# Two graph attentions on one core: the end of the first one, with norm weights folded into matrices and evictions moved between engines

## The chip, the cores and the metric

The kernel runs on one core of one Trainium2 chip. A core has four compute engines with an instruction queue each, worked off in order: TensorE (PE in the profile; its weight loads are PEld), VectorE (DVE), ScalarE (ACT) and GpSimd (POOL). SyncE (SP) only issues DMAs here. Engines wait for each other through semaphores. The metric is the device time of one execution in microseconds, and the median of several.

## The reference

A graph of N = 1250 nodes and E = 20000 edges, with 768 features a node, goes through two graph layers, each behind a layer norm and a residual. The first layer holds two attentions (GATv2), and the change touches the passage from one to the other:

```python
def gatv2(x, src, dst, Ws, bs, Wd, bd, attn):        # attn: H heads x D
    fs = (x @ Ws + bs).reshape(-1, H, D)
    fd = (x @ Wd + bd).reshape(-1, H, D)
    e = leaky_relu(fs[src] + fd[dst], 0.2)
    logits = einsum('ehd,hd->eh', e, attn)
    ex = exp(logits - segment_max(logits, dst)[dst])
    alpha = ex / segment_sum(ex, dst)[dst]
    return elu(segment_sum(alpha[:, :, None] * fs[src], dst))

h   = gatv2(x, src, dst, W1s, b1s, W1d, b1d, attn1)   # 8 heads of 96
h   = layer_norm(h + x, ln1_w, ln1_b)                 # (v - mean) * rsqrt(var + eps) * w + b
out = gatv2(h, src, dst, Wos, bos, Wod, bod, attno)   # 1 head of 768
x   = layer_norm(out, lno_w, lno_b)
```

Here `x` is max(norm(input), 0), and the result is added to the input. The second layer is a relational graph convolution (34 relations, each with a 768 x 768 matrix) followed by a graph convolution; the change does not touch it.

## The kernel before

**Stages.** By the profile's times: edge lists and the two products of the first attention up to about 260 us, the first attention to about 905, the second to 1370, the relations to 2567, the graph convolution to the end at 2808.5. The stages follow each other, since each reads tables that the last tile of the stage ahead has written.

**Tiles and slots.** Nodes are sorted by their number of incoming edges and cut into ten tiles of 128 (`k` = 0 to 9). Tile k has as many slots as its busiest node has edges: 33, 22, 20, 18, 17, 16, 15, 14, 13 and 11, 179 in all. A slot is one incoming edge of each of the 128 nodes. Tiles of over 20 slots are worked in two chunks.

**A slot** has a front and a back. The front (`front`): POOL gathers the 128 source rows by an indirect DMA into one of a ring of 24 buffers (L1145, `fs<-f_fs_d` in the first attention, `fs<-r_fs_d` in the second). VectorE takes `z = max(fs, nfd)` (L1205), multiplies by the attention vector (L1210) and sums by head (L1211). Leaky relu is split there: 0.2 (fs + fd) is linear, so its sum with the attention vector comes with the source row, in extra columns ("quarter sums", because SLOPE / (1 - SLOPE) is 0.25), and the rest is 0.8 max(fs + fd, 0), which is 0.8 (max(fs, -fd) + fd). `nfd` is the tile's -fd; its own sums are the same for all edges of a node, and the softmax takes them out. The back (`back`): ScalarE scales the gathered row by the softmax weight, one instruction for each of eight heads (L1263), and TensorE adds it to the tile's PSUM sum by two matmuls with the identity (L1265, `ag`). A buffer of the ring is free again when the ag matmuls of its slot are done. The loop at the foot of `attention` works the back of one chunk and the front of the next side by side; `softmax` stands between them (exponential L1229).

**POOL's second work.** With each gather of the first attention, 0.9 scatters of list records are issued (L1149, `r_pair_d<-rec,place`); what is left over of the 179, up to 60, follows the last gather. The relations read these lists.

**A tile's beginning.** `negated1`, called one chunk or two ahead, gathers the nodes' own rows h0, transposes them, multiplies by W1d (L1114, PSUM tag mm2) and evicts `nfd = -(product + b1d)` on VectorE (L1409).

**A tile's end.** `end` multiplies the sum by 1/denominator (`share`) and takes elu (L1288 to L1290). Then `finish1`, as long as the change finds it:

```python
            nc.vector.tensor_add(o, o, h0s.pop(k))
            sc, sh = norm_scale(nc, small, f, o, P)
            nc.scalar.activation(o, o, AF.Identity, bias=sh, scale=sc)        # L1418
            nc.vector.tensor_mul(o, o, lnw)                                   # L1419
            nc.vector.tensor_add(o, o, lnb)                                   # L1420
            ...
            nc.vector.tensor_add(halves(fs, P, f), ps[:, :, :HW], halves(bias_s, P, f))    # L1426
            ...
            nc.vector.scalar_tensor_tensor(wt, fs[:, :D], SLOPE / (1.0 - SLOPE), attn_o, op0=ALU.mult, op1=ALU.mult,
                                           accum_out=fs[:, D:])               # L1428
```

The normed rows are transposed on TensorE (`to_columns`), multiplied by Wos, evicted with the bias into `fs2` (one buffer) with the quarter sum as a 769th column, and scattered by POOL into the table `r_fs_d` of the second attention (L1149, `r_fs_d<-fs,f_perm`). Then the product with Wod is evicted as `-(product + bod)` on VectorE (L1433) and stored by SyncE. All products of `negated1` and `finish1` use one PSUM buffer, mm2.

**The weights.** `loads1` is called at the front of the fourth slot: Wos and Wod come by SyncE's queue (issued at 239.0 and 239.5 us), the rows lnw, lnb, bias_s, bias_d and attn_o, each spread over 128 partitions, by ScalarE's.

**Order.** The order in each engine's queue is not written out by hand: a scheduler merges the instruction streams, so instructions of `finish1`, of slots and of `negated1` interleave on each engine.

Of the kernel before, what the change touches and what calls it, by code (L numbers as in the profile page):

```python
# [10 lines left out]
F32 = mybir.dt.float32  # L11
# [3 lines left out]
AF = mybir.ActivationFunctionType  # L15
ALU = mybir.AluOpType
AX = mybir.AxisListType

P = 128
# [606 lines left out]
def fast_front(ctx, tc, f, x, src, dst, edge_type, W1s, b1s, W1d, b1d, attn1, attno, W_rel):  # L626
# [51 lines left out]
    with ExitStack() as front:  # L678
# [33 lines left out]
        ones_row = early.tile([1, P], F32, name="ones_row")  # L712
# [10 lines left out]
        f.bias_1 = const.tile([P, D], F32, name="bias_1")  # L723
        nc.scalar.dma_start(f.bias_1, bass.AP(tensor=b1d.tensor, offset=b1d.offset, ap=[[0, P], [1, D]]))
# [352 lines left out]
def halves(t, n, f):  # L1077
    return t[:n, :f.D].rearrange("p (a b) -> p a b", a=2)
# [45 lines left out]
def fast_rest(ctx, tc, f, x, src, dst, edge_type, W1s, b1s, W1d, b1d, attn1, ln1_w, ln1_b,  # L1124
# [44 lines left out]
    def attention(H, table, negated, attn_e, first, loads, finish, rate, rest):  # L1169
# [98 lines left out]
        def share(o, ps, by):  # L1268

            if H == 1:  # L1270
                nc.vector.tensor_scalar(halves(o, P, f), ps[:, :, :HW], by, None, op0=ALU.mult)
            else:
                nc.vector.tensor_tensor(
                    o.rearrange("p (a h d) -> p a h d", a=2, d=HD),
                    ps[:, :, :HW].rearrange("p a (h d) -> p a h d", d=HD),
                    by.rearrange("p (a h) -> p a h", a=2)[:, :, :, None].to_broadcast([P, 2, H // 2, HD]),
                    op=ALU.mult)

        def end(t):
# [4 lines left out]
            share(o, c.ps, c.den)  # L1284
# [3 lines left out]
            nc.vector.tensor_scalar(e, o, 0.0, None, op0=ALU.min)  # L1288
# [31 lines left out]
        for j, now in enumerate(chunks):  # L1320
# [13 lines left out]
            if now.first + now.n == now.t.S:  # L1334
# [7 lines left out]
                            f.degf[:, :, None].to_broadcast([P, NT, S0]), op=ALU.is_ge)  # L1342

# [46 lines left out]
    with ExitStack() as one:  # L1390
        bias_1 = f.bias_1
# [10 lines left out]
        def negated1(k, nfd):  # L1402

            h0s[k] = pool.tile([P, D], F32, name="h0", tag="h0r", bufs=3)
            gather(h0s[k], f.h0_d[:, :], f.permg[:, k:k + 1])
            hT = pool.tile([P, KC, P], F32, name="hT0", tag="hT1", bufs=1)
            to_columns(nc, ps_t, f, hT, 0, h0s[k], P, both=True)
            ps = dense(nc, ps_t, f, hT, f.w1d, 0, P, tag="mm2")
            nc.vector.scalar_tensor_tensor(  # L1409
                nfd.rearrange("p (a h) d -> p a h d", a=2), ps[:, :, :HW].rearrange("p a (h d) -> p a h d", d=D // H),  # L1410
                -1.0, bias_1.rearrange("p (a h d) -> p a h d", a=2, d=D // H), op0=ALU.mult, op1=ALU.subtract)

        def finish1(k, o):
            lnw, lnb, wos, wod = late["lnw"], late["lnb"], late["wos"], late["wod"]
            bias_s, bias_d, attn_o = late["bias_s"], late["bias_d"], late["attn_o"]
# [3 lines left out]
            nc.vector.tensor_mul(o, o, lnw)  # L1419
            nc.vector.tensor_add(o, o, lnb)  # L1420
            hT = pool.tile([P, KC, P], F32, name="hT1", tag="hT1", bufs=1)
            to_columns(nc, ps_t, f, hT, 0, o, P)
            ps = dense(nc, ps_t, f, hT, wos, 0, P, tag="mm2")
            ap1 = late["pool"]
            fs = ap1.tile([P, W2], F32, name="fs2", tag="fs2", bufs=1)
            nc.vector.tensor_add(halves(fs, P, f), ps[:, :, :HW], halves(bias_s, P, f))  # L1426
            wt = work.tile([P, D], F32, name="wt2", tag="att_e")
            nc.vector.scalar_tensor_tensor(wt, fs[:, :D], SLOPE / (1.0 - SLOPE), attn_o, op0=ALU.mult, op1=ALU.mult,  # L1428
                                           accum_out=fs[:, D:])
# [3 lines left out]
            nc.vector.scalar_tensor_tensor(halves(fd, P, f), ps[:, :, :HW], -1.0, halves(bias_d, P, f),  # L1433
                                           op0=ALU.mult, op1=ALU.subtract)
# [5 lines left out]
    with ExitStack() as two:  # L1440
# [34 lines left out]
        attention(1, fs2_d, negated2, f.attn_o, lambda: None, loads2, finish2, 0, 0)  # L1475
# [239 lines left out]
```

## Time and profile before

| what | us |
|---|---|
| median of three runs | 2816.5 (2815.39 to 2821.32) |
| the profiled execution | 2810.31 |
| its span | 2808.5 |
| granted TensorE clock, mean | 0.932 of full speed |
| first attention, tiles running | 263 to 873 |
| of its 610 us busy: PE, DVE, ACT, POOL | 488.3, 538.6, 418.4, 477.0 |
| last list scatter of the first attention to the first gather of the second | 872.7 to 905.9 |

The slices of the page cut the span into 40 equal parts of 70 us; a digit is the busy share in tenths, 9 for 90% and more:

```profile
PE   6942684789898386889599999999999999997998
DVE  5579979898994999999463433343333333310000
ACT  3003774776762122333212122212212212221000
POOL 1332877787884776776374555455455544421000
```

The first attention is the stretch of the fourth to the thirteenth digit, in which all four engines are in use; the second attention follows with a busy DVE; in the relations PE is the one at 9. A group line has the line of the code, engine, operation, output and inputs with their shapes, and a count; then the sum and the mean in us and ns; then the idle time just ahead of the group's instructions and what ended it. A timeline line begins with its start and its length in us. Register, semaphore and DMA-issuing instructions do not count as busy. All times that follow are of this profiled execution, which lies 6.2 us below the median.

### The profile page before, as it was taken

To read this page: it belongs to the slowest core of one execution; us is meant where nothing else is said; L and a number is where in the kernel's file an instruction comes from. 1 tells how busy PE (TensorE), PEld (TensorE's weight loads), DVE (VectorE), ACT (ScalarE), POOL (GpSimd) and SP (SyncE) were. 2 spreads that over 40 slices of the span, in tenths; PEclk is the share of its full clock that TensorE was granted. 3 is DMA by queue.
4 is the path that set the end of the run, shared out by engine and by line. 5 is a ranking of instruction groups with operands and counts; after the bars stand their busy time and mean duration, and the time that the engine had idled before them with its cause. 6 is when DMAs were issued, how large, how long until landed. Compare 5 with 4: busy or idle time off the path is not lost. (4 is left out here: it accounts for less than half of the span.)

```text
span 2808.5 us, 24226 instructions
## 1 busy us (share of the span) xinstructions
PE 2396.5 (85%) x7859; PEld 1395.3 (50%) x7859; DVE 1615.1 (58%) x2382; ACT 852.6 (30%) x2340; POOL 1471.1 (52%) x1039
## 2 busy tenths in 40 slices
PE   6942684789898386889599999999999999997998
PEld 3521252445454243545366666666666666664455
DVE  5579979898994999999463433343333333310000
ACT  3003774776762122333212122212212212221000
POOL 1332877787884776776374555455455544421000
PEclk9976997999999698999799999999999999999999
DMA  6144443444431766675477777777677777665211
GB/s 213 46 157 156 134 132 91 125 145 134 133 97 53 277 206 189 212 220 169 169 196 214 191 185 197 184 187 186 181 201 186 184 201 198 174 147 136 75 45 51
DMA packets 130769, 447.82 MB, mean 159 GB/s; under 512 B 25016, under 2 KB 27601, under 8 KB 130634
## 3 DMA queue, kind: packets, MB, share of 16 engines
q0 software_dynamic: 77792, 305.26, 41.7%
q1 hardware_dynamic: 48041, 133.96, 13.4%
q10 hardware_dynamic: 4800, 6.96, 0.7%
q8 instruction: 65, 1.06, 0.2%
q14 instruction: 71, 0.57, 0.1%
HBM read 357.08 MB, written 89.11 MB: 159 GB/s over the span
## 5 line engine op out<-in xcount | busy, mean ns | idle before, releaser
L1114 PE MATMUL ps<-wrel,mT 128*128 128x384 f32 x3336 | 1099.4, 486 | 1.2 <-DMA wrel<-in_L_gnn_W_rel_dram 1.2
L1114 PEld LDWEIGHTS ps<-wrel,mT 128*128 128x128 f32 x3336 | 623.2, 190 | 407.4 <-issue 1.5
L1145 POOL DMA_INDIRECT g<-r_h_d,lists x241 | 365.9, 1518 | 474.1 <-DVE g L1566 302.3
L1265 PE MATMUL ag<-fs,identf 128*128 128x384 f32 x716 | 290.2, 539 | 173.2 <-ACT fs L1263 163.4
L1263 ACT ACTIVATE fs<-fs,lg 128x96 f32<-128x96 f32 x1376 | 370.6, 362 | 2.4 <-issue 1.9
L1566 DVE TENSOR_TENSOR g<-g,g 128x768 f32<-128x768 f32 x68 | 64.6, 949 | 526.4 <-DMA g<-r_h_d,lists 464.7
L1205 DVE TENSOR_TENSOR z<-fs,nfd 128x776 f32<-128x776 f32 (+1 forms) x358 | 344.0, 976 | 39.6 <-DMA fs<-f_fs_d,srci 22.6
L1255 PE MATMUL ag<-fs,dg 128*128 128x384 f32 x716 | 252.3, 514 | 86.2 <-ACT dg L1253 45.9
L1145 POOL DMA_INDIRECT fs<-f_fs_d,srci x179 | 245.9, 1374 | 103.1 <-issue 47.2
L1592 POOL DMA_INDIRECT r_h_d<-y,lists x139 | 227.3, 1635 | 133.1 <-ACT y L1591 65.8
L1149 POOL DMA_INDIRECT r_pair_d<-rec,place x179 | 240.9, 1346 | 101.3 <-DVE lg L1211 48.6
L1265 PEld LDWEIGHTS ag<-fs,identf 128*128 128x128 f32 x716 | 135.2, 204 | 315.7 <-ACT fs L1263 247.5
L1145 POOL DMA_INDIRECT fs<-r_fs_d,srci x179 | 242.5, 1355 | 82.6 <-PE ag L1255 35.5
L1506 DVE SCALAR_TENSOR_TENSOR arow<-node,from_f,arow 128x1250 f16<-128x1250 f16 x179 | 270.7, 1514 | 3.7
L1255 PEld LDWEIGHTS ag<-fs,dg 128*128 128x128 f32 x716 | 142.9, 202 | 190.8 <-ACT dg L1253 91.1
L1591 ACT COPY y<-ps 128x768 f32<-128x768 f32 x71 | 56.8, 799 | 482.0 <-PE ps L1114 482.0
L1589 ACT ACTIVATE y<-ps,rcnt 128x768 f32<-128x768 f32 x68 | 61.3, 902 | 444.4 <-PE ps L1114 444.4
L1207 DVE SCALAR_TENSOR_TENSOR z<-z,attn_o 128x769 f32<-128x769 f32 x179 | 180.2, 1027 | 0.0
L1210 DVE TENSOR_TENSOR z<-z,attn 128x776 f32<-128x776 f32 x179 | 168.3, 954 | 0.1
L1211 DVE TENSOR_REDUCE lg<-z 128x8 f32<-128x776 f32 x179 | 167.9, 950 | 0.1
L1647 DVE COPY gT<-hb 128x512 f32<-128x512 f32 (+1 forms) x9 | 5.4, 603 | 250.0 <-ACT gT L1646 250.0
L1643 PE MATMUL hb<-adj,h 125*128 125x512 f32 (+1 forms) x360 | 130.9, 526 | 14.6 <-DMA h<-r_h_d 14.6
(274 smaller groups left out, 2269.7 us busy)
## 6 DMA issues: line engine op xcount, KB each, us to landing
wrel<-in_L_gnn_W_rel_dram SPq DMA_DIRECT2D x37, 2304.0 KB
g<-r_h_d,lists POOLq DMA_INDIRECT x241
r_nfd_d<-fd SPq DMA_DIRECT2D x10, 384.0 KB
nfd<-r_nfd_d SPq DMA_DIRECT2D x10, 384.0 KB
r_x_d<-xb SPq DMA_DIRECT2D x10, 384.0 KB
x1r<-r_x_d SPq DMA_DIRECT2D x10, 384.0 KB
f_fs_d<-o_s SPq DMA_DIRECT2D x9, 388.0 KB
x<-in_x_dram SPq DMA_DIRECT2D x9, 384.0 KB
```

Source lines behind the costliest of these rows:

```text
L1114: last = nc.tensor.matmul(ps[:n, half, :f.HW], hT[:, k, j * P:j * P + n], w[:, k, cols], start=(k == 0), stop=(k == f.KC - 1 and not bias))
L1145: return nc.gpsimd.indirect_dma_start(out=to, out_offset=None, in_=table, in_offset=bass.IndirectOffsetOnAxis(ap=idx, axis=0))
L1149: s = nc.gpsimd.indirect_dma_start(out=table, out_offset=bass.IndirectOffsetOnAxis(ap=idx, axis=0), in_=rows, in_offset=None, **kw)
L1205: nc.vector.tensor_tensor(z, fs, t.nfd, op=ALU.max)
L1207: nc.vector.scalar_tensor_tensor(z[:, 0, :], z[:, 0, :], 1.0, attn_e[:, 0, :], op0=ALU.mult, op1=ALU.mult, accum_out=t.lg[:, s, :])
L1210: nc.vector.tensor_mul(z, z, attn_e)
L1211: nc.vector.tensor_reduce(t.lg[:, s, :], z, axis=AX.X, op=ALU.add)
L1255: nc.tensor.matmul(c.ps[:, half, :HW], dg, fs[:, 0, half * HW:(half + 1) * HW], start=begin, stop=end)
L1263: nc.scalar.activation(fs[:, h, :HD], fs[:, h, :HD], AF.Copy, scale=t.lg[:, s, h:h + 1])
L1265: nc.tensor.matmul(c.ps[:, half, :HW].rearrange("p (h d) -> p h d", d=HD), f.identf, fs[:, half * H // 2:(half + 1) * H // 2, :HD], start= ...
L1506: nc.vector.scalar_tensor_tensor(a, node16, from_f[:, k, s:s + 1], a, op0=ALU.is_equal, op1=ALU.add)
L1592: s = nc.gpsimd.indirect_dma_start(out=h1_d[:, :], out_offset=bass.IndirectOffsetOnAxis(ap=j.node, axis=0), in_=y, in_offset=None, compute ...
```

## The change

The norm of the first attention, `w * n + b` with n the plain normed row, is followed only by the products with Wos and Wod. So w can be multiplied into the rows of the two matrices once, and b becomes a row, `b @ W`, that joins the layer's own bias. The change does this in `loads1`, on the loaded matrices: ScalarE scales their blocks, TensorE computes the bias rows. The bias of the source product (`bos + b @ Wos`) is not added to the rows of the table any more; since the softmax weights of a node sum to one, it is added after the weighted sum, in the second attention's `share`, and it cancels from the logits but for the maximum: as it stands within max(fs, -fd), it goes into the destination's bias, by the third product below (`sums[:, 0]`). The quarter sums become a 769th column of Wos (six sums on VectorE, once). A node without edges would have the bare bias now, so the second attention's norm is multiplied by a 0/1 column (`f.has`). The evictions of nfd, fs (in halves) and fd go from VectorE to ScalarE, and the biases of nfd and fd come as one more matmul of a ones row for each half.

```diff
-        f.bias_1 = const.tile([P, D], F32, name="bias_1")
+        f.bias_1 = const.tile([1, D], F32, name="bias_1")
...
-        def share(o, ps, by):
+        def share(o, ps, by, bias=None):
-            if H == 1:
+            if bias is not None:
+                nc.vector.scalar_tensor_tensor(halves(o, P, f), ps[:, :, :HW], by, halves(bias, P, f),
+                                               op0=ALU.mult, op1=ALU.add)
+            elif H == 1:
...
+    f.has = rp.tile([P, NT], F32, name="has")
+    nc.vector.tensor_scalar(f.has, f.degf, 0.5, None, op0=ALU.is_gt)
...
         def loads1():
-            late["wos"], late["wod"] = load_w(ap1, Wos, "wos", "wos"), load_w(ap1, Wod, "wod", "wod")
-            for name, a in (("lnw", ln1_w), ("lnb", ln1_b), ("bias_s", bos), ("bias_d", bod), ("attn_o", attno)):
-                late[name] = load_row(ap1, a, name)
+            wos = late["wos"] = ap1.tile([P, KC, W2], F32, name="wos")
+            nc.sync.dma_start(wos[:, :, :D], Wos.rearrange("(k p) n -> p k n", p=P))
+            wod = late["wod"] = load_w(ap1, Wod, "wod", "wod")
...
+            for i, a in enumerate((ln1_w, ln1_b)):
+                nc.scalar.dma_start(cols[:, i, :], bass.AP(tensor=a.tensor, offset=a.offset, ap=[[1, P], [P, KC]]))
+            for i, a in enumerate((bos, bod)):
+                nc.scalar.dma_start(rows[:, i, :], bass.AP(tensor=a.tensor, offset=a.offset, ap=[[0, 1], [1, D]]))
+            late["bias_d"] = sums[:, 1, :]
+            for i, w in enumerate((wos, wod)):
+                ps = ps_t.tile([P, 2, 512], F32, name="b_ps", tag="mm2")
+                for half in range(2):
+                    at = slice(half * HW, (half + 1) * HW)
+                    for k in range(KC):
+                        nc.tensor.matmul(ps[:1, half, :HW], cols[:, 1, k:k + 1], w[:, k, at], start=(k == 0), stop=False)
+                    if i:
+                        nc.tensor.matmul(ps[:1, half, :HW], f.ones_row[:, :1], sums[:, 0, at], start=False, stop=False)
+                    nc.tensor.matmul(ps[:1, half, :HW], f.ones_row[:, :1], rows[:, i, at], start=False, stop=True)
+                nc.scalar.copy(sums[:, i, :].rearrange("p (a b) -> p a b", a=2), ps[:1, :, :HW])
+                for k in range(KC):
+                    nc.scalar.activation(w[:, k, :D], w[:, k, :D], AF.Copy, scale=cols[:, 0, k:k + 1])
+            ps = ps_t.tile([P, 2, 512], F32, name="b_ps", tag="mm2")
+            for half in range(2):
+                nc.tensor.matmul(ps[:, half, :HW], f.ones_row, sums[:, 0, half * HW:(half + 1) * HW], start=True, stop=True)
+            nc.scalar.copy(halves(f.bias_s, P, f), ps[:, :, :HW])
+            for k in range(KC):
+                wt = work.tile([P, D], F32, name="wt2", tag="att_e")
+                nc.vector.scalar_tensor_tensor(wt, wos[:, k, :D], SLOPE / (1.0 - SLOPE), f.attn_o[:, 0, :D],
+                                               op0=ALU.mult, op1=ALU.mult, accum_out=wos[:, k, D:])
...
-            ps = dense(nc, ps_t, f, hT, f.w1d, 0, P, tag="mm2")
-            nc.vector.scalar_tensor_tensor(
+            ps, _ = dense(nc, ps_t, f, hT, f.w1d, 0, P, tag="mm2", bias=(f.ones_row, f.bias_1))
+            nc.scalar.activation(
                 nfd.rearrange("p (a h) d -> p a h d", a=2), ps[:, :, :HW].rearrange("p a (h d) -> p a h d", d=D // H),
-                -1.0, bias_1.rearrange("p (a h d) -> p a h d", a=2, d=D // H), op0=ALU.mult, op1=ALU.subtract)
+                AF.Copy, scale=-1.0)
...
-            nc.vector.tensor_mul(o, o, lnw)
-            nc.vector.tensor_add(o, o, lnb)
...
-            nc.vector.tensor_add(halves(fs, P, f), ps[:, :, :HW], halves(bias_s, P, f))
-            wt = work.tile([P, D], F32, name="wt2", tag="att_e")
-            nc.vector.scalar_tensor_tensor(wt, fs[:, :D], SLOPE / (1.0 - SLOPE), attn_o, op0=ALU.mult, op1=ALU.mult,
-                                           accum_out=fs[:, D:])
+            for half in range(2):
+                at = slice(half * HW, HW if half == 0 else W2)
+                for c in range(KC):
+                    nc.tensor.matmul(ps[:, half, :at.stop - at.start], hT[:, c], wos[:, c, at], start=(c == 0), stop=(c == KC - 1))
+                nc.scalar.copy(fs[:, at], ps[:, half, :at.stop - at.start])
...
-            ps = dense(nc, ps_t, f, hT, wod, 0, P, tag="mm2")
+            ps, _ = dense(nc, ps_t, f, hT, wod, 0, P, tag="mm2", bias=(f.ones_row, late["bias_d"]))
...
-            nc.vector.scalar_tensor_tensor(halves(fd, P, f), ps[:, :, :HW], -1.0, halves(bias_d, P, f),
-                                           op0=ALU.mult, op1=ALU.subtract)
+            nc.scalar.activation(halves(fd, P, f), ps[:, :, :HW], AF.Copy, scale=-1.0)
...
+            for a in (sc, sh):
+                nc.vector.tensor_mul(a, a, f.has[:, k:k + 1])
```

More of the change, by code (lines that the diff above doesn't have):

```diff
@@ L711, in fast_front @@
         nc.scalar.dma_start(bias1[:, :, :HW], bass.AP(tensor=b1s.tensor, offset=b1s.offset, ap=[[0, 1], [HW, 2], [1, HW]]))
-        ones_row = early.tile([1, P], F32, name="ones_row")
+        ones_row = f.ones_row = const.tile([1, P], F32, name="ones_row")
         nc.vector.memset(ones_row, 1.0)
@@ L722, in fast_front @@
         f.attn_1 = by_heads(attn1, "attn_1")
-        f.bias_1 = const.tile([P, D], F32, name="bias_1")
-        nc.scalar.dma_start(f.bias_1, bass.AP(tensor=b1d.tensor, offset=b1d.offset, ap=[[0, P], [1, D]]))
+        f.bias_1 = const.tile([1, D], F32, name="bias_1")
+        nc.scalar.dma_start(f.bias_1, bass.AP(tensor=b1d.tensor, offset=b1d.offset, ap=[[0, 1], [1, D]]))
+        f.bias_s = const.tile([P, D], F32, name="bias_s")
         f.attn_o = by_heads(attno, "attn_o")
@@ L1167, in fast_rest, with attention @@
     RW = D + H
-    def attention(H, table, negated, attn_e, first, loads, finish, rate, rest):
+    def attention(H, table, negated, attn_e, first, loads, finish, rate, rest, bias=None):
         HD = D // H
@@ L1283, in end @@
             e = work.tile([P, D], F32, name="att_e", tag="att_e")
-            share(o, c.ps, c.den)
+            share(o, c.ps, c.den, bias)
             if len(t.done) > 1:
@@ L1390, in fast_rest @@
     with ExitStack() as one:
-        bias_1 = f.bias_1
         late = {}
@@ new lines, in loads1 @@
+            wod = late["wod"] = load_w(ap1, Wod, "wod", "wod")
+            cols = ap1.tile([P, 2, KC], F32, name="ln_cols")
+            rows = ap1.tile([1, 2, D], F32, name="b_rows")
+            sums = ap1.tile([1, 2, D], F32, name="b_sums")
+            for i, a in enumerate((ln1_w, ln1_b)):
+                nc.scalar.dma_start(cols[:, i, :], bass.AP(tensor=a.tensor, offset=a.offset, ap=[[1, P], [P, KC]]))
+            for i, a in enumerate((bos, bod)):
+                nc.scalar.dma_start(rows[:, i, :], bass.AP(tensor=a.tensor, offset=a.offset, ap=[[0, 1], [1, D]]))
@@ L1407, in negated1 @@
             to_columns(nc, ps_t, f, hT, 0, h0s[k], P, both=True)
-            ps = dense(nc, ps_t, f, hT, f.w1d, 0, P, tag="mm2")
-            nc.vector.scalar_tensor_tensor(
+            ps, _ = dense(nc, ps_t, f, hT, f.w1d, 0, P, tag="mm2", bias=(f.ones_row, f.bias_1))
+            nc.scalar.activation(
                 nfd.rearrange("p (a h) d -> p a h d", a=2), ps[:, :, :HW].rearrange("p a (h d) -> p a h d", d=D // H),
-                -1.0, bias_1.rearrange("p (a h d) -> p a h d", a=2, d=D // H), op0=ALU.mult, op1=ALU.subtract)
+                AF.Copy, scale=-1.0)
         def finish1(k, o):
-            lnw, lnb, wos, wod = late["lnw"], late["lnb"], late["wos"], late["wod"]
-            bias_s, bias_d, attn_o = late["bias_s"], late["bias_d"], late["attn_o"]
+            wos, wod, ap1 = late["wos"], late["wod"], late["pool"]
             nc.vector.tensor_add(o, o, h0s.pop(k))
@@ L1418, in finish1 @@
             nc.scalar.activation(o, o, AF.Identity, bias=sh, scale=sc)
[L1419 to L1420 removed]
             hT = pool.tile([P, KC, P], F32, name="hT1", tag="hT1", bufs=1)
             to_columns(nc, ps_t, f, hT, 0, o, P)
[L1423 to L1424 removed]
+            ps = ps_t.tile([P, 2, 512], F32, name="ps", tag="mm2")
             fs = ap1.tile([P, W2], F32, name="fs2", tag="fs2", bufs=1)
[L1426 to L1429 removed]
+            for half in range(2):
[3 more added lines that the diff above has]
+                nc.scalar.copy(fs[:, at], ps[:, half, :at.stop - at.start])
             scatter(fs2_d[:, :], fs, f.perm[:, k:k + 1], "fs2")
[L1431 removed]
+            ps, _ = dense(nc, ps_t, f, hT, wod, 0, P, tag="mm2", bias=(f.ones_row, late["bias_d"]))
             fd = ap1.tile([P, D], F32, name="fd2", tag="fd2", bufs=1)
[L1433 to L1434 removed]
+            nc.scalar.activation(halves(fd, P, f), ps[:, :, :HW], AF.Copy, scale=-1.0)
             nc.sync.dma_start(nfd2_d[k * P:(k + 1) * P, :], fd)
@@ L1473, in negated2 @@
             nc.sync.dma_start(nfd[:, 0, :], nfd2_d[k * P:(k + 1) * P, :])
-        attention(1, fs2_d, negated2, f.attn_o, lambda: None, loads2, finish2, 0, 0)
+        attention(1, fs2_d, negated2, f.attn_o, lambda: None, loads2, finish2, 0, 0, f.bias_s)
     both.close()
```

## The prediction

> **What bounds the kernel now.** The page's slices show where the stages change; a table of windows, one stage per row and columns as in its first line, then shows what limits each.
>
> ```profile
> core 0: us, PE busy (x) PEld busy (x) DVE busy (x) ACT busy (x) POOL busy (x), PEclk, DMA share, GB/s
> 263.00:873.00 610.00, 488.28 (x1411) 259.22 (x1410) 538.61 (x746) 418.40 (x1444) 477.00 (x346) 0.91 0.41 117
> 910.00:1370.00 460.00, 342.02 (x1003) 198.00 (x1004) 428.50 (x816) 133.09 (x273) 318.07 (x225) 0.86 0.64 202
> ```
>
> The change lies in the first row, the first attention; the later stages start when it ends, so what it gains or loses reaches the end. VectorE is busy 538.6 of 610 us (88%). POOL's 477.0 us hide more: its groups in that window show a gap ahead of nearly every instruction.
>
> ```profile
> L1149 POOL DMA_INDIRECT r_pair_d<-rec,place x176 | 237.3, 1348 | 53.6 <-issue 47.5 <-DMA fs<-f_fs_d,srci 1.8 <-DVE lg L1211 1.5
> L1145 POOL DMA_INDIRECT fs<-f_fs_d,srci x155 | 222.3, 1434 | 95.8 <-PE ag L1265 41.8 <-issue 40.1 <-ACT fs L1263 9.6
> ```
>
> 346 gaps of 0.30 us (as in the lines below) are 103.8 us; with them POOL is taken 581 of 610 us, 95%. Its instructions are long for a reason the timeline shows:
>
> ```profile
> 268.35 3.64 POOL L1145 DMA_INDIRECT fs<-f_fs_d,srci  x1 [0.30 <-issue]
> 272.29 0.99 POOL L1149 DMA_INDIRECT r_pair_d<-rec,place  x1 [0.30 <-DVE lg L1211]
> 267.54 1.83 DVE L1205 TENSOR_TENSOR z<-fs,nfd 128x776 f32<-128x776 f32 x2
> 269.30 1.83 DVE L1210 TENSOR_TENSOR z<-z,attn 128x776 f32<-128x776 f32 x2
> 271.05 1.81 DVE L1211 TENSOR_REDUCE lg<-z 128x8 f32<-128x776 f32 x2
> ```
>
> An indirect DMA takes 0.99 us beside VectorE's reduce and 3.64 us when it meets z and the multiplication, which read two SBUF tiles. 346 at 0.97 would be 336 us: 141 us are stretch. So VectorE and POOL limit each other: z waited for gathered rows 18 times, 22.6 us. The list of waits also gives ScalarE 85.8 us of waiting for att_e (it is not a bound: 418 of 610 us), TensorE 109.4 us for ScalarE's scalings, VectorE 21.8 us in three waits for nfd's product.
>
> **What the Trainium skill says.** "SBUF — State Buffer", section "Who interferes with whom": a VectorE instruction with two SBUF inputs contends with a GpSimd instruction that reads SBUF, one with at most one SBUF input doesn't. The 3.64 against 0.99 us agree, though the page infers that a tensor_tensor leaves descriptor generation alone; here the trace decides. "DMA: Bandwidth & Descriptors", section "Specifications": transfers under 512 B don't reach line rate. The two new column loads are 768 pieces of 4 B each; the nearest row, a load of 1280 pieces of 16 B, was issued at 100.86 and read at 103.38, 2.5 us.
>
> **The change part by part.** Times are against the profiled execution, 2810.3 us (span 2808.5 and 1.8 around it), 6.2 below the median 2816.5.
>
> (a) VectorE loses six instructions a tile:
>
> ```profile
> L1419 DVE TENSOR_TENSOR att_o<-att_o,lnw 128x768 f32<-128x768 f32 x7 | 6.6, 944 | 0.0
> L1420 DVE TENSOR_TENSOR att_o<-att_o,lnb 128x768 f32<-128x768 f32 x7 | 6.6, 945 | 0.0
> L1426 DVE TENSOR_TENSOR fs<-ps,bias_s 128x768 f32<-128x768 f32 x7 | 6.6, 944 | 0.0
> L1428 DVE SCALAR_TENSOR_TENSOR wt<-fs,attn_o 128x768 f32<-128x768 f32 x7 | 6.6, 943 | 0.0
> L1433 DVE SCALAR_TENSOR_TENSOR fd<-ps,bias_d 128x768 f32<-128x768 f32 x7 | 6.7, 951 | 0.0
> L1409 DVE SCALAR_TENSOR_TENSOR nfd<-ps,bias 128x768 f32<-128x768 f32 x6 | 5.7, 952 | 12.0 <-PE ag L1265 9.7 <-issue 2.3
> ```
>
> 0.944 + 0.945 + 0.944 + 0.943 + 0.08 (the sum's write) + 0.951 + 0.952 = 5.76 us, 57.6 for ten tiles. Only lnw, lnb and wt (2.9 us a tile) read two SBUF tiles; the other three read PSUM and were open windows for POOL. Where VectorE runs without a gap (415 to 495) POOL got one instruction a slot through in 2.3 us and needs 1.9 a slot. So where POOL sets the pace the open windows come back as VectorE waits. There the gain is only the stretch of the closed ones: 141 us of stretch over 155 x 1.93 + 9 x 2.83 = 325 us of such work is 0.43, x 2.9 = 1.3 us a tile; at most all 2.9. Where VectorE is gapless it is 5.76 less small gaps, 4.4 to 5.3. I take 1.3 for five of the ten tiles and about 2.6, halfway, for the other five: -19. Ends: -50 (the first rival) and +5 (a POOL that loses more windows than it gains).
>
> (b) ScalarE gains nfd, fs in two halves and fd a tile. PSUM evictions of this width on it (y, 799 ns) give 0.8 + 0.8 + 2 x 0.48 = 2.6 us, 26 over 192 us idle: no bound. But its queue is in order, and a slot's eight scalings are 8 x 0.266 = 2.13 us. Each eviction may stand behind a slot, the second half of wos's product now waits for the first half's copy, and behind it on TensorE stand wod's product and the ag matmuls that free gather buffers. TensorE has 122 us idle of 610, 12 a tile, and before it waited likewise for VectorE's eviction in a queue of 2.8 us a slot; so I take nothing. Ends: -5 (quicker than VectorE), and one slot's wait at each of the two evictions that others queue behind (fs's first half, nfd), 4.3 us a tile less half a slot of VectorE's, 1.4, that it waited before: 2.9 a tile, +29. TensorE's four bias matmuls a tile, some 0.33 us each, 1.3 us, fit in its idle time; without that cover 13. nfd's copy for the last tiles comes behind up to 30 scalings (8 us) while VectorE already waited 5.46 us there:
>
> ```profile
> 806.13 0.96 DVE L1409 SCALAR_TENSOR_TENSOR nfd<-ps,bias 128x768 f32<-128x768 f32 x1 [5.46 <-PE ag L1265]
> ```
>
> That is why late tiles get no full gain in (a).
>
> (c) Once, at the start: the folding. wos lands about 248 and wod 254 (issued at 239.0 and 239.5, 4.7 MB at 292 to 404 GB/s). TensorE sums 28 bias rows, ScalarE scales 12 blocks (0.93 to 1.03 us) and copies three results, VectorE makes six sums (0.95) just after the first softmax instruction. Before, the exponential ran at 258.63, and then:
>
> ```profile
> 258.97 34.10 ACT L1263 ACTIVATE fs<-fs,lg 128x96 f32<-128x96 f32 x128
> 263.40 3.35 POOL L1145 DMA_INDIRECT fs<-f_fs_d,srci  x1 [25.69 <-PE ag L1265]
> ```
>
> In the changed order the exponential follows wos's scaling and sums (about 262), and wod's six scalings and a copy stand within slot 0's scalings: 5.5 to 7 us more before the first buffer is freed. The gather of 263.4, which had waited 25.7 us for it, starts at 271 to 273.5: +8, ends +4 and +14. Nothing hides it: the ring of 24 is full. The five row loads left out had time anyway: 0.
>
> (d) The tail of the last tile, a plain chain:
>
> ```profile
> 872.71 0.96 POOL L1149 DMA_INDIRECT r_fs_d<-fs,f_perm  x1 [0.30 <-issue]
> 875.84 0.96 DVE L1426 TENSOR_TENSOR fs<-ps,bias_s 128x768 f32<-128x768 f32 x1 [10.42 <-DMA r_fs_d<-fs,f_perm]
> 877.72 0.55 DVE L1288 TENSOR_SCALAR att_e<-att_o 128x768 f32<-128x768 f32 x1
> 901.97 0.96 POOL L1149 DMA_INDIRECT r_fs_d<-fs,f_perm  x1 [22.87 <-DVE wt L1428]
> 905.94 0.98 POOL L1145 DMA_INDIRECT fs<-r_fs_d,srci  x1 [3.01 <-DMA r_fs_d<-fs,f_perm]
> ```
>
> POOL's list scatters run to 872.7; the second-last tile's fs waits for the one fs2 buffer, and the last tile's elu queues behind it on VectorE: 33.2 us to the next gather. Now that fs waits on ScalarE, so elu (1.9) doesn't queue behind it, and lnw, lnb, wt (2.8) and fs + half a copy (about 1.8) go: -6.5, ends -9 and -2.
>
> (e) Second attention: two tiny multiplications a tile (0.15 each, 3.0 in all) beside a VectorE 93% busy, less the share with bias for the one without (0.95 for 1.006 us, -0.6 for ten) and a few waits: +1.5, ends 0 and +4. The bias itself rides on the share at no instruction.
>
> Sum: -19 + 0 + 8 - 6.5 + 1.5 = -16. Profiled run 2794; from the median, 2816.5 - 16 = 2800.5.
>
> **The rivals.** First, VectorE alone is the bound: all of (a), 57.6 less the 6 us it waits anyway, is won, -50 + 8 - 6.5 + 1.5 = -47, 2769. For it: 88% busy, and 415 to 495 gapless. Against: POOL 95% taken, and three of six instructions were POOL's windows. Second, POOL is the whole bound: then (a) gives 0 to -6, and (c) to (e), 8 - 6.5 + 1.5 = +3, so 0 on average, -3 to +3, about 2816. For it: the gaps; against: 41.8 us in which POOL itself waited for buffers. Third, slower: ScalarE's in-order queue, between the halves of wos's product and at nfd. At (b)'s upper end, 2.9 us a tile, -16 + 29 = +13, 2829.5. For it: TensorE already waits 109.4 us for ScalarE, in which these copies are to stand. Against: ScalarE has 192 us idle, and 24 buffers lie between a late ag matmul and a late z. It decides from 1.6 us a tile, a tenth of the 16 gained.
>
> **How the numbers follow.** Forecast 0.48, VectorE's bound 0.20, POOL's bound 0.13, slower 0.19. The forecast's own range, 2786 to 2815, takes (a)'s gain from 10 to 30 us and (c) from +4 to +14; the whole range goes to 2767, which takes in more than half of the first rival, and to 2823, the POOL rival and a third of the slower one. 0.2% is 5.6 us, about what a measurement can tell from no change. Faster: 0.45 + 0.20 + 0.01 = 0.66; same 0.03 + 0.11 + 0.01 = 0.15; slower 0.01 + 0.18 = 0.19.
>
> **What would show it.** Right: first gather after the ring's wait at 271 to 273; POOL's mean in the steady window below 1.38 us but VectorE's waits for gathered rows above 22.6; VectorE's busy time there down by about 55 and the window by 15 to 25 only; 26 to 28 us from the last list scatter to the next gather. Wrong: steady window down by 45 or more (first rival), or TensorE's wait for ScalarE's scalings and nfd's waits growing by more than 60 us (third).

## The result and the profile after

The changed kernel takes 2858.2 us (median of five, 2852.24 to 2881.41), the kernel before 2817.9 in runs beside it: a ratio of 1.0155, interval 1.0131 to 1.0179. It is 40 us slower, where 16 us faster was forecast and 2823 was the end of the range. The experiments ran on several chips. On some the kernel before takes 2794 us and the changed one 2824 (ratio 1.0101, interval 1.0077 to 1.0125), on the others 2807 to 2819 and 2849 to 2858, so ratios are compared, or profiles of one chip where there are such.

The profiled execution of the changed kernel (2881.4 us) was the longest of its five, by 20 us: from 857 to 889 us only POOL works in it, with no wait that the profile shows. In no other profile of the kernel does this come again, so the readings below use others where that stretch matters. The table has stage lengths from three profiles taken on one chip, in us; "first z" is the first instruction of a slot on VectorE, "elu" its first instruction at a tile's end.

| stage | before | changed | changed without bias matmuls |
|---|---|---|---|
| first z to tile 0's elu | 156.7 | 174.5 | 177.0 |
| tile 0's elu to tile 7's elu | 460.7 | 475.6 | 456.3 |
| tile 7's elu to the second attention's first gather | 94.3 | 94.5 | 95.8 |
| from there to the last elu | 445.4 | 450.9 | 454.4 |
| last elu to the end | 1462.9 | 1459.9 | 1462.1 |

The changed kernel loses 17.8 us at the start, 14.9 in the tile loop and 5.5 in the second attention, and gets 3.6 back ahead of the first z and after the last elu: 34.8 in all, 2813.7 to 2848.6. In its other profiles the loop took 462 to 465 us, and the kernel before had 457 to 468 there in other profiles; so the loop is level or up to 15 us longer, and nowhere shorter by the 19 us expected. On the faster chips the kernel before was not profiled. Its time there, less the stages as other profiles have them (185 us to the first z, 156 to tile 0's elu, 96 for the tail, 445 and 1461 behind), leaves about 450 us for its loop, an estimate, where the changed kernel had 462 and 463.

The window of the tiles in the changed kernel's first profile and then of the one taken beside the runs of the third group below (columns as in the first line; the second is from a faster chip, where the window holds more of the tiles' work):

```profile
core 0: us, PE busy (x) PEld busy (x) DVE busy (x) ACT busy (x) POOL busy (x), PEclk, DMA share, GB/s
263.00:873.00 610.00, 490.78 (x1409) 251.77 (x1407) 477.84 (x662) 430.17 (x1434) 426.21 (x332) 0.90 0.42 116
```
```profile
263.00:873.00 610.00, 518.13 (x1503) 271.84 (x1502) 498.69 (x691) 443.74 (x1491) 449.67 (x343) 0.93 0.42 117
```

VectorE fell from 538.6 to 478 or 499, POOL from 477.0 to 426 or 450: the instructions are gone, and POOL isn't stretched more. As the windows don't hold the same work, the loop of the table (tile 0's to tile 7's elu, one chip) is the better measure: VectorE's busy time goes from 405.2 to 368.8 us there, and TensorE's from 368.1 to 398.1, with 368.0 where the bias matmuls are left out. POOL with a gap of 0.30 us for each of its 343 instructions is taken 553 of 610 us in the second line, 91% where it was 95. What replaced the work is waiting. POOL's groups in the second of these profiles, then VectorE's waits there (us in total, times, longest):

```profile
L1150 POOL DMA_INDIRECT r_pair_d<-rec,place x174 | 227.1, 1305 | 53.0 <-issue 46.3 <-DMA fs<-f_fs_d,srci 2.4 <-DMA r_pair_d<-rec,place 1.5
L1146 POOL DMA_INDIRECT fs<-f_fs_d,srci x155 | 204.2, 1318 | 135.3 <-PE ag L1266 89.0 <-issue 36.8 <-ACT nfd L1443 1.9
```
```profile
DVE z L1206 <- DMA fs<-f_fs_d,srci: 44.7, 27, 7.5
DVE z L1206 <- ACT nfd L1443: 42.8, 4, 21.2
```

POOL's instructions became a little shorter (1434 to 1318 ns, 1348 to 1305), as the coupling with VectorE would have it. Yet gathers wait 89.0 us for ag matmuls to free a buffer (41.8 before). Of these, 46.1 are the ring's first wait at the start (25.7 before); in the loop it is 40.4 against 13.0. And z waits 44.7 us for rows (22.6) and 42.8 for nfd, whose product VectorE waited 24.1 for before. Both ways lead to TensorE: there the path has to be looked for.

What changed shows in TensorE's timeline of one tile's end. First before, then after (the profile beside the third group); an FP32 matmul makes two records, and a line of the code has a number a little higher in the changed kernel (the ag matmuls are L1266 there, L1265 before):

```profile
543.68 7.90 PE L1114 MATMUL ps<-wos,hT 128*128 128x384 f32 x24
551.42 2.10 PE L1265 MATMUL ag<-fs,identf 128*128 128x384 f32 x6
553.36 7.90 PE L1114 MATMUL ps<-wod,hT 128*128 128x384 f32 x24
561.10 4.03 PE L1265 MATMUL ag<-fs,identf 128*128 128x384 f32 x12
```
```profile
550.28 4.03 PE L1115 MATMUL ps<-wod,hT 128*128 128x384 f32 x12
554.24 0.91 PE L1119 MATMUL ps<-b_sums,ones_row 1*128 1x384 f32 x2
555.08 4.14 PE L1115 MATMUL ps<-wod,hT 128*128 128x384 f32 x12
559.15 0.91 PE L1119 MATMUL ps<-b_sums,ones_row 1*128 1x384 f32 x2
559.99 5.43 PE L1266 MATMUL ag<-fs,identf 128*128 128x384 f32 x16
...
575.42 0.91 PE L1119 MATMUL ps<-bias,ones_row 1*128 1x384 f32 x2
576.26 8.98 PE L1266 MATMUL ag<-fs,identf 128*128 128x384 f32 x27
```

A product of 24 records is one block in TensorE's queue, and no ag matmul comes between. It took 7.9 us and now takes 9.7 (550.28 to 559.99), for each half ends with a bias matmul of 0.91. With nfd's product the tile has two such blocks, 3.6 us. The gathers behind them show it in POOL's timeline of the same profile, where waits of this kind before, at 553.88 and 577.40 us, were 0.30:

```profile
561.82 0.99 POOL L1146 DMA_INDIRECT fs<-f_fs_d,srci  x1 [3.67 <-PE ag L1266]
577.95 0.99 POOL L1146 DMA_INDIRECT fs<-f_fs_d,srci  x1 [6.04 <-PE ag L1266]
```

There is a second way, without the ring: z of the next tile waits for nfd, which comes out of such a block. The wait as tile 6 ends, with the bias matmuls and then without them and the fold (e3_no_fold_no_bias), on one chip:

```profile
756.57 1.84 DVE L1206 TENSOR_TENSOR z<-fs,nfd 128x776 f32<-128x776 f32 x2 [8.69 <-ACT nfd L1443]
723.75 1.85 DVE L1206 TENSOR_TENSOR z<-fs,nfd 128x776 f32<-128x776 f32 x2 [6.12 <-ACT nfd L1424]
```

### The profile page after: what moved, and what is told of

Same layout as the page of the kernel before. It is cut to its first block, busy times and chain, and to the rows that moved or that the text cites. A ratio compares the mean times of both kernels' runs of the same rounds, so it can differ in the third digit from the quotient of the medians.

```text
span 2879.6 us, 24520 instructions
## 1 busy us (share of the span) xinstructions
PE 2451.4 (85%) x8003; PEld 1410.0 (49%) x8003; DVE 1574.6 (55%) x2345; ACT 889.5 (31%) x2395; POOL 1428.4 (50%) x1039
## 5 line engine op out<-in xcount | busy, mean ns | idle before, releaser
L1206 DVE TENSOR_TENSOR z<-fs,nfd 128x776 f32<-128x776 f32 (+1 forms) x358 | 351.4, 997 | 115.2 <-DMA fs<-f_fs_d,srci 44.3
L1266 PE MATMUL ag<-fs,identf 128*128 128x384 f32 x716 | 278.8, 528 | 98.2 <-ACT fs L1264 82.1
L1146 POOL DMA_INDIRECT fs<-f_fs_d,srci x179 | 229.3, 1281 | 156.6 <-PE ag L1266 96.2
L1150 POOL DMA_INDIRECT r_pair_d<-rec,place x179 | 218.7, 1222 | 100.2 <-issue 50.0
L1266 PEld LDWEIGHTS ag<-fs,identf 128*128 128x128 f32 x716 | 135.2, 201 | 230.0 <-ACT fs L1264 124.3
L1208 DVE SCALAR_TENSOR_TENSOR z<-z,attn_o 128x769 f32<-128x769 f32 x179 | 172.6, 987 | 0.0
```

The lines of the kernel that those rows point to most:

```text
L1146: return nc.gpsimd.indirect_dma_start(out=to, out_offset=None, in_=table, in_offset=bass.IndirectOffsetOnAxis(ap=idx, axis=0))
L1150: s = nc.gpsimd.indirect_dma_start(out=table, out_offset=bass.IndirectOffsetOnAxis(ap=idx, axis=0), in_=rows, in_offset=None, **kw)
L1206: nc.vector.tensor_tensor(z, fs, t.nfd, op=ALU.max)
L1208: nc.vector.scalar_tensor_tensor(z[:, 0, :], z[:, 0, :], 1.0, attn_e[:, 0, :], op0=ALU.mult, op1=ALU.mult, accum_out=t.lg[:, s, :])
L1266: nc.tensor.matmul(c.ps[:, half, :HW].rearrange("p (h d) -> p h d", d=HD), f.identf, fs[:, half * H // 2:(half + 1) * H // 2, :HD], start= ...
```

## The experiments

The expectations name four theories of the loss. S: the folding at the start costs it. Q: the evictions in ScalarE's in-order queue do. P: the bias matmuls in TensorE's queue do; it came with the second group, after Q had fallen. V is the prediction's rival of a POOL that bounds. Runs whose names begin alike (e1, e2 and so on) are of one group; the groups e1 and e3 ran on faster chips.

**Once more (e1_again).** 

> The changed kernel once more, for one profile. In its first profile every engine but POOL stands still from 857 to 889 us, while POOL issues the last list scatters, and this execution was 23 us longer than the median of the other four. If the standstill belongs to the kernel, it shows again with about 30 us; if it is an accident of one execution, the stretch from tile 8's transposes to its product with Wos takes under 8 us and the time is about 2857. The first exponential (268.6) and the first gather after the ring's wait should come at the same places in either case.

2824.9 us, one run, on a faster chip. From 857 to 889 all engines worked: the standstill was an accident of one execution. The first gather after the ring's wait came at 268.6.

**The folding later (e1_late_fold).** The fold is cut off `loads1` and queued on TensorE behind the last ag matmul of the first chunk:

```diff
+                if later and j == 0 and i == now.n - 1:
+                    back(now, i)
+                    with tc.issue_after(f.ag.ins):
+                        later()
```

> The same work, but TensorE's bias rows, and with them ScalarE's scalings of the weights and VectorE's six sums, come after the ag matmuls of the first chunk. Theory S (the start: folding ahead of the first exponential and the first scalings holds back the first free gather buffer): exponential back at about 259, first gather after the ring's wait about 264, tile 0's elu near 358 instead of 373, and 12 to 20 us less than the changed kernel, about 2840. Theory Q (ScalarE's queue at the tiles' ends): the first tiles come earlier but the later ones catch no more than 5 us of it, about 2853.

2819.5 us, 1.0085 (1.0063 to 1.0108), 5 us less than the changed kernel on that kind of chip (2824.0), which the intervals don't tell apart. The first gather came 18 us earlier (250.0), but tile 0's elu 2 us later (352.1 against 350.1 in e1_again, on the same chip). Theory S in this form is wrong: most of the cost stays when the place is changed. The six sums on VectorE now stand ahead of the second chunk's maximum and its exponential, and TensorE's bias rows ahead of that chunk's ag matmuls.

**No folding at all (e1_no_fold_work).** 

> Leaves out the folding itself: no bias rows on TensorE, no scaling of the weights, no quarter sums (the column is zero); the two bias rows are loaded as they are. The rest of the changed kernel stays. Theory S: the whole cost of the start goes, 18 to 25 us less than the changed kernel, about 2836. Theory Q: at most 10 us less, 2848 or more. What then remains above the kernel before belongs to the tiles' ends, the tail and the second attention.

2806.7 us, 1.0037 (1.0026 to 1.0048): 17 us less than the changed kernel, 12 above the kernel before. The work of the fold costs 17 us where it stands, and 13 in the other place. By the profiles 14 of the 17 lie ahead of tile 0's elu (150.4 us after the first z, against 164.7).

**Evictions on VectorE (e1_evict_dve).**

```diff
-            nc.scalar.activation(halves(fd, P, f), ps[:, :, :HW], AF.Copy, scale=-1.0)
+            nc.vector.tensor_scalar(halves(fd, P, f), ps[:, :, :HW], -1.0, None, op0=ALU.mult)
```

and nfd and fs likewise. 

> The folding stays, but nfd, fs in halves and fd are evicted by VectorE. Theory Q: the waits of z for nfd on ScalarE (40.6 us in three) and the ring's waits go, 15 to 35 us less than the changed kernel in spite of 28 us more work on VectorE, 2825 to 2842. Theory S: VectorE gets 2.8 us a tile back and the start stays, 0 to 20 us more than the changed kernel, 2857 to 2877.

2827.2 us, 1.0115 (1.0093 to 1.0137): the same as the changed kernel within 3 us. Evictions on ScalarE don't cause the loss, and 28 us of VectorE work more cost nothing either: VectorE, idle for 94 of the 463 us of the changed kernel's loop, is not its bound. By single profiles the nothing is a sum: the loop took 468 us against 462, the tail 92.6 against 99.1.

**No bias matmuls (e2_no_bias_mm).**

```diff
-            ps, _ = dense(nc, ps_t, f, hT, wod, 0, P, tag="mm2", bias=(f.ones_row, late["bias_d"]))
+            ps = dense(nc, ps_t, f, hT, wod, 0, P, tag="mm2")
```

and nfd's product likewise. 

> The changed kernel without the bias matmuls of nfd's and fd's products; it leaves out these two biases. Theory P (TensorE bounds the tiles now: a product with bias takes it 10.0 us in one block instead of 8.0, in its queue ahead of the ag matmuls that free gather buffers): four matmuls of 0.91 us a tile go, 20 to 35 us less than the changed kernel. Theory V (POOL's instructions bound the tiles in both kernels): 0 to 5 us less, for TensorE's time was idle time.

2835.9 us, 1.0066 (1.0041 to 1.0090), on a slower chip, where the changed kernel stood at 1.0155. Tile 0's to tile 7's elu took 443 us, against 472 in the profile of the next run, which has the matmuls. That is 25 us by the ratios, within theory P's 20 to 35. That run:

**No mask (e2_no_has).** 

> The changed kernel without the 20 small multiplications of the second attention; it leaves out the mask for nodes without edges. If these stand on VectorE's path there, 3 to 7 us less than the changed kernel, and the second attention from its first gather to its last elu takes 445 instead of 452 us. If the longer second attention comes from something else, under 2 us.

2853.9 us, 1.0123 (1.0097 to 1.0150). Its interval overlaps that of the changed kernel, but the stage agrees with the first case: 447.0 us from first gather to last elu, where the changed kernel had 451 to 452 in four profiles. So about 5 us by that stage, for 20 instructions of 0.15. A profile of the kernel before on this chip (e2_before) had 445.4.

**The matmuls alone (e3_pe_bias_only).** From the kernel before, with nothing folded:

```diff
-            ps = dense(nc, ps_t, f, hT, f.w1d, 0, P, tag="mm2")
-            nc.vector.scalar_tensor_tensor(
+            ps, _ = dense(nc, ps_t, f, hT, f.w1d, 0, P, tag="mm2", bias=(f.ones_row, f.bias_1))
+            nc.scalar.activation(
...
+                AF.Copy, scale=-1.0)
```

and fd likewise. 

> From the kernel before, this part of the change alone: nfd's and fd's biases as matmuls on TensorE, and their evictions on ScalarE. VectorE loses 1.9 us a tile, TensorE gains 3.6. Theory P (a product with bias blocks TensorE's queue 1.8 us longer, ahead of the ag matmuls): 5 to 20 us slower than before although VectorE was busy 88%. If the evictions on VectorE were on the path: 5 to 15 us faster.

2808.9 us, 1.0056 (1.0039 to 1.0073): 15 us slower than before, by this part alone, although it takes 1.9 us a tile off an engine that was busy 88%. Its tile loop took 471 us, where about 450 were estimated above for the kernel before on such a chip. The part has evictions on ScalarE in it, which cost nothing in sum in e1_evict_dve; so the matmuls remain.

**Both costs out (e3_no_fold_no_bias), beside the changed kernel (e3_after).** 

> The changed kernel without both: no folding at the start (no bias rows, no scaling, quarter sums zero) and no bias matmuls in nfd's and fd's products; it leaves out these parts of the computation. If the two costs add (18 us for the folding, 20 to 25 for the matmuls), it is 38 to 43 us below the changed kernel and near or up to 10 us below the kernel before. If they hide one another it is 25 us below the changed kernel or less.

2788.9 us, 0.9982 (0.9973 to 0.9990), with the changed kernel at 2824.0: 35 us below it and 4.9 below the kernel before. The two costs add to 34 to 42 us by the runs that took one out (17 for the fold, 17 to 25 for the matmuls), so they hardly hide one another, though 35 is a little under the 38 expected. The loop took 443.0 us; with the matmuls and without the fold (e1_no_fold_work) it took 461.0.

**Norm as columns (e2_columns, e3_columns).** From the kernel before; weight and bias are applied in the copies out of PSUM, where a feature is a partition, and the quarter sums are a column of Wos:

```diff
+            for c in range(3):
+                w, b = affine[:, 0, g + c:g + c + 1], affine[:, 1, g + c:g + c + 1]
+                if g == 0:
+                    nc.scalar.activation(hT[:, g + c, :n], ptv[:, c, :n], AF.Identity, bias=b, scale=w)
+                else:
+                    nc.vector.tensor_scalar(hT[:, g + c, :n], ptv[:, c, :n], w, b, op0=ALU.mult, op1=ALU.add)
...
-            nc.vector.tensor_mul(o, o, lnw)
-            nc.vector.tensor_add(o, o, lnb)
...
-            wt = work.tile([P, D], F32, name="wt2", tag="att_e")
+            nc.vector.tensor_copy(fs[:, D:], ps[:, 1, HW:HW + 1])
```

> From the kernel before: the norm's weight and bias are applied as columns while the transposed rows are copied out of PSUM (six copies of 128 columns instead of two of 384), and the quarter sums are a column of Wos, summed once late in the second chunk; biases and evictions stay as before. VectorE loses the three instructions a tile that read two SBUF tiles, TensorE gains nothing. Theory P: 15 to 30 us faster than the kernel before, for the gain in VectorE and POOL time isn't taken back by TensorE. Theory V: 10 to 15 us (1.3 us of POOL's stretch a tile). If a chain through the tile's end bounds: within 5 us of before.

2807.1 us against 2819.0, 0.9960 (0.9944 to 0.9975); beside the changed kernel, on the faster chip, 2784.4, 0.9959 (0.9944 to 0.9974). It beats both kernels: no norm weight is folded into matrices, TensorE gets no matmul more, and the three instructions that read two SBUF tiles are gone. In its timeline the products are short again:

```profile
528.93 7.98 PE L1121 MATMUL ps<-wod,hT 128*128 128x384 f32 x24
536.75 7.26 PE L1272 MATMUL ag<-fs,identf 128*128 128x384 f32 x22
```

It gains 9 to 12 us, not the 28 of the removed instructions. That is V's number (10 to 15), not P's (15 to 30): with no bias matmul in the way, most of VectorE's gain is still taken back.

**No list scatters, before (e4_before_no_lists).** 

> The kernel before without the list scatters (179 of POOL's instructions); it leaves out the lists, so the relations read rows of zeros. POOL's bound (theory V): the tile loop loses most of POOL's 141 us of stretch, tile 2's period falls from 66 to under 60, and the time falls by the tail's 20 to 25 us and 20 us or more from the loop, 40 to 60 in all. If a chain through TensorE's queue and the ring bounds: the tail's 20 to 25 us and under 10 from the loop.

2795.8 against 2817.3, 0.9912 (0.9883 to 0.9940), 21 to 25 us. Most is in the loop: 442 us from tile 0's to tile 7's elu, 15 to 25 less than with lists; 7 more lie ahead of tile 0's elu. The tail stayed (96 us from there to the next gather), against both theories, and in all it is half of what V expected (40 to 60). POOL is part of the bound, but with its instructions halved (346 to 170) the loop got only 3 to 5% shorter, and its gathers waited for TensorE instead:

```profile
L1145 POOL DMA_INDIRECT fs<-f_fs_d,srci x155 | 251.7, 1624 | 273.2 <-PE ag L1265 157.3 <-DVE z L1205 78.7 <-issue 22.8
```

**No list scatters, without the two costs (e4_rest_no_lists).** 

> The changed kernel without folding, without bias matmuls and without the list scatters; it leaves out these parts. With POOL out of the way VectorE's 58 us less should show if POOL was what took them: theory V 30 to 45 us below the kernel before without lists. If TensorE's queue and the ring bound: 5 to 15 us below it, as with lists (4.9 below, of which the second attention's multiplications hide about 6).

2774.6, 0.9847 (0.9822 to 0.9872), 21 us below the kernel before without lists, where the same pair with lists is 4.9 apart. Neither theory's number is met. By stages of the two profiles (24.7 us apart) it is 11 in the loop (442 to 431), 14 in the tail (96 to 82), less 5 in the second attention, and 5 in the rest. So the list scatters hid the tail's gain; in the loop, VectorE's 40 us less over seven tiles give 11 even with half of POOL's instructions gone, so POOL is hardly what took the rest.

**Lists moved on (e4_columns_lists).** `finish1, 0.9, 0` and `finish2, 0.3, 60` in the two calls of `attention`. 

> The columns version, with the 36 list scatters that are left over after the last gather spread over the second attention (0.3 with each gather) instead of standing ahead of the last rows' scatter. If they set the tail: the first gather of the second attention comes 25 us after the last tile's elu instead of 40, and 8 to 15 us less than the columns version (0.9959), 0.990 to 0.993 of before. If the second attention pays for them: the same as the columns version within 3 us.

2824.3, 1.0028 (1.0017 to 1.0039), 19 us worse than the columns version. The tail did shrink (from the last elu to the next gather 30.5 us against 42), but the second attention, whose VectorE is busy 93% before, grew from 445 to 474.

**Three profiles on one chip (e5_before, e5_after, e5_no_bias_mm)** gave the table at the head. 

> The changed kernel on the same chip: 9 to 18 us more up to tile 0's elu, the tile loop 0 to 10 us more than before if the bias matmuls take back all that VectorE gained, the tail 0 to 3 more, the second attention 6 to 7 more. If the loop is shorter than before by over 5 us, the matmuls take back less than was said.

 

> The changed kernel without the bias matmuls of nfd's and fd's products (it leaves out these biases) on the same chip: start and second attention as the changed kernel, the tile loop 15 to 22 us shorter than the changed kernel's.

The loop was 14.9 us longer than before, not 0 to 10, and 19.3 shorter without the bias matmuls.

## Why the prediction was wrong

**(b) The matmuls: the step that failed.** The prediction put "TensorE's four bias matmuls a tile, some 0.33 us each, 1.3 us" into TensorE's idle time, at no cost. Both halves fail. The four took 3.6 us. The group of wod's bias over seven tiles, and then one such matmul in the kernel before, in the products ahead of the first attention:

```profile
L1119 PE MATMUL ps<-b_sums,ones_row 1*128 1x384 f32 x28 | 12.7, 534 | 0.0
101.75 0.91 PE L812 MATMUL ps<-bias,ones_row 1*128 1x388 f32 x2
```

28 records for 14 matmuls: two each, 0.534 us a record, no cheaper than those of 128 rows (0.49). The 0.33 is 7.90 / 24, one record's share of a product, and a matmul makes two; before's own trace had the price, 0.91 us. The Trainium skill, "TensorE: Matmul & The Clock Gate", section "Why this matters for your kernels", says that a single matmul with K (the rows summed over) of 32 takes the time of one with K of 128; in the trace a K of 1 takes no less than one of 128 either. And the 20% of idle time were not where the matmuls went. By three pairs of profiles their 3.6 us a tile cost 18 to 29 us over the loop's seven tiles (19.3 in the table), 2.6 to 4.2 a tile, and alone they turn a relief of VectorE into a loss of 15 us.

That they cost this is shown; by which way is read from waits. One is the circle ag matmul, free buffer, gather, z, softmax, scaling, ag matmul, in which the block stands; the other is nfd, which z waits for directly. From e1_no_fold_work to e3_no_fold_no_bias, which differ by these matmuls alone, z's waits for rows in the loop fall from 39.5 to 26.9 us. Those for nfd fall from 42.5 to 14.1, but a wait of 17.6 for ag matmuls stands where one of 21.1 for nfd stood. So the rows give 12.6 us and nfd 10.8, about equal shares. No run took out one of the two pairs of matmuls, or let ag matmuls in between, so which block counts, and whether its length or TensorE's time as such, stays open. The prediction asked of TensorE only how busy it was.

**(a) VectorE and POOL: right in kind, the size unproven.** The gain was put at -19 of a possible 57.6. Without the two costs it appears as -4.9 us net, of which the second attention's multiplications hide 5; about -10 then, and -9 to -12 for the columns. The coupling of VectorE and POOL is there (POOL's instructions got shorter), but it is hardly what takes the gain in the loop: without lists the loop gives 11 of 40. A part of the rest can be seen. In e3_no_fold_no_bias the copy of fd waits at the head of ScalarE's queue for wod's product, and the next softmax's exponential, ready to run, stands behind it:

```profile
770.20 0.81 ACT L1445 ACTIVATE fd<-ps 128x768 f32<-128x768 f32 x1 [8.10 <-PE ps L1115]
773.07 0.29 ACT L1230 ACTIVATE lg<-lg 128x104 f32<-128x104 f32 x1
773.39 0.34 DVE L1232 TENSOR_REDUCE den<-lg 128x8 f32<-128x104 f32 x1 [9.21 <-ACT lg L1230]
```

VectorE's waits for the exponential come to 13.2 us in that loop. In all profiles with evictions on ScalarE they are 3.8 to 19.0 us, with all of them on VectorE 0.4 to 1.6. For what is left, the circle through TensorE is the likely reading, not shown: no run shortened that circle alone.

**(c) The start: a term left out, the size half.** The first gather was to move by 8. In three profiles of the changed kernel the first z stood 83.2 or 83.3 us ahead of the first freed gather (80.8 in a fourth), 66.4 and 66.5 before: +16.8. The prediction walked ScalarE's queue and gave TensorE's bias rows no time (it counts 28; there are 30, and two matmuls of the third product). But ScalarE can scale a matrix in place only when TensorE has read it, and the first ag matmul stands behind all these rows. Of the first profile, TensorE and then ScalarE:

```profile
252.92 6.21 PE L1418 MATMUL b_ps<-wos,ln_cols 128*1 128x384 f32 x12 [59.39 <-DMA b_rows<-in_L_gnn_bod_dram]
...
270.94 4.03 PE L1418 MATMUL b_ps<-wod,ln_cols 128*1 128x384 f32 x12
...
276.27 0.91 PE L1266 MATMUL ag<-fs,identf 128*128 128x384 f32 x2
```
```profile
268.57 0.31 ACT L1230 ACTIVATE lg<-lg 128x128 f32<-128x128 f32 x1 [0.88 <-DVE lg L1229]
271.78 5.07 ACT L1424 ACTIVATE wod<-wod,ln_cols 128x768 f32<-128x768 f32 x6 [1.44 <-PE b_ps L1418]
277.43 1.70 ACT L1264 ACTIVATE fs<-fs,lg 128x96 f32<-128x96 f32 x6
```

23.4 us pass from the first bias row to the first ag matmul. The exponential came at 268.57 instead of about 262. The wait for TensorE, wod's scalings and the copy then held up slot 0's own scalings for 7.1 us (270.35 to 277.43), about as forecast, and the buffer was freed by the slot's second ag matmul at 280.22. "Nothing hides it" holds for the most part: against the run without the fold the first freed gather came 19.5 us later (83.3 against 63.8 us after the first z) and tile 0's elu 14.3. On the faster chips that stage is only 8.5 us longer than in the columns version (164.6 against 156.1), close to the 8 forecast; but there the rest of the change gains about 6 (150.4 without the fold), so the agreement is luck.

**(d) The tail: no gain.** -6.5 was forecast. From the row scatter right behind the last list scatter (872.71 in the profile before; the last list scatter itself ran at 871.43) to the next gather it is 33.2 and 34.8 us in two profiles before, 34.8 to 39.2 in three of the changed kernel, and the table has +0.2. VectorE's queue was indeed freed, but the wait moved on. Of ScalarE's timeline there:

```profile
879.52 0.48 ACT L1460 COPY fs<-ps 128x384 f32<-128x384 f32 x1 [13.17 <-DMA r_fs_d<-fs,f_perm]
880.02 1.28 ACT L1090 ACT_TABLE_LOAD   x1
881.32 0.29 ACT L1090 ACTIVATE rs<-mv,f_eps_col 128x1 f32<-128x1 f32 x1
```

fs of the second-last tile waits 13.2 us for the one buffer, and behind it on ScalarE stands the square root of the last tile's norm, which VectorE then waits 12.0 us for. A gain appears only without the list scatters that keep the buffer busy (14 us in one pair of profiles, above). The forecast named what queued behind the waiting instruction on the engine it left, and didn't ask the same of the engine it went to.

**(e) The second attention: 1.5 forecast, 5.5 to 7.6 measured.** 20 small multiplications at 0.15 us make 3.0; that they also lie in the chain of each tile's norm is the likely reason. The run without the mask gives back about 5.

**The rivals.** The third, slower, had the right sign and, in the main, the wrong engine. Neither of its signs came: TensorE's wait for ScalarE's scalings fell from 109.4 to 73.1 us, nfd's waits grew by 19, not 60; and evictions back on VectorE changed nothing in sum. What it says of the in-order queue is there, at the exponential. VectorE alone as the bound is out. POOL alone as the bound is out too: with half its instructions gone the loop lost 3 to 5%.

**What stays open.** On the slower chips the changed kernel loses 40 us, on the faster 30. In all five profiles on slower chips of versions with the fold in its own place, ScalarE's scalings at 290 to 375 us have gaps, 7.8 to 10.2 us in all, for which the profile shows no wait; in none of the kernel before or the columns there, and not on the faster chips. This fits the difference in sign and most of its size; its cause wasn't found.

## What to carry to other kernels

Price a matmul by what the trace shows for its columns and type, whatever the rows: here a bias by a ones row added 0.84 us to a block in which a full step of the product takes 0.66 (7.90 / 12), and "the engine is only 80% busy" didn't hide it, since the queue is in order and others wait for what stands behind or comes out. A copy that waits at the head of such a queue holds up what stands behind it, too. Before moving work between engines, follow the circle that frees buffers and ask of each engine on it how long its longest uninterrupted block is. An affine map by feature can ride on a copy out of PSUM that has the feature on its partitions: no matrix has to be scaled and no bias row summed, and here that version was 0.4% faster than the kernel before.

## What the runs showed of the hardware

A matmul with one row of contraction took two records of 0.534 us, one with 128 rows two of 0.49, both with 384 columns in FP32; six with a single output row took 4.03 us, as long as six with 128 rows out (4.03 to 4.14). POOL's gathers got shorter beside a VectorE with fewer instructions that read two SBUF tiles (1434 to 1318 ns); but in the loop without bias matmuls they took 1145 ns, 1336 with them on the same chip, at the same VectorE work, so the number of these instructions isn't all that counts. And 36 list scatters moved beside a VectorE that was busy 93% lengthened that stage by 29 us, 0.8 us each.
